# A graph attention layer on one core: queries projected inside the walk instead of ahead of it

## The chip, the core and the metric

The kernel runs on one core of a Trainium2 chip, one launch, all tensors in float32 in device memory. The metric is device time in microseconds (us) from launch to end. The core has five engines that run their own instruction queues in order: TensorE (PE in the profile, with its weight loads as PEld), VectorE (DVE), ScalarE (ACT), GpSimd (POOL) and SyncE (SP, which here only issues transfers). They meet through semaphores.

## What is computed

One pre-normalised graph attention layer over 12500 nodes with 256 features, 8 heads of 32, and 200000 edges sorted by destination:

```python
h = jnp.maximum(_layernorm(x, axis=-1), 0.0)          # 12500 x 256
q, k, v = h @ Wq + bq, h @ Wk + bk, h @ Wv + bv       # each 8 heads of 32
logits = einsum('ehd,ehd->eh', q[dst], k[src]) / sqrt(32)
expv = exp(logits - segment_max(logits, dst)[dst])
agg = segment_sum(expv / segment_sum(expv, dst)[dst] * v[src], dst)
out = agg + (h @ Wskip + bskip)
y = h + gelu(out)
return x + layernorm(y) * gamma + beta
```

The destinations are drawn as `12500 * u**2` and sorted, so low nodes have many edges and high nodes few: 383 edges in a row span up to 26 nodes in the first half of the list and up to 53 in the second.

## The kernel before

**Projection** (`project`, L112). The nodes are cut into 98 blocks of 128 rows, taken in 14 groups of 7. For a block the statistics are made on DVE, the centred and clipped rows are transposed on PE (L95) and copied to SBUF by ACT (L97), and PE multiplies them with `[Wk Wv]` (L161, 512 columns) and with `Wq` (L164, 256 columns). DVE scales the two results by the row's reciprocal deviation and adds the bias (L167, L169). A group's rows go to the device-memory tables `kv_tab` (2 KB a row), `q_tab` (1 KB a row) and `st_tab` (L172).

**Plan** (`make_plan`, L291). Beside the projection, mostly on DVE, the edge list is cut into `S` = 8 streams of about 25000 edges and each stream into `NST` = 66 steps of 384 edges (`K` = 3 pieces of 128, one edge of overlap). Out come the gather indices `idx`, the first node of every step and stream (`d0_row`), rows from which one-hot matrices are made (`e_tab`), penalties for the maxima (`pen_tab`), and a list of output blocks in the order in which they become complete (`slot_row`, two blocks make a pair, 52 pairs). A flag says whether the data fit: no step of a stream may reach further than its window (64 nodes, `WN`), and a block must be complete when its pair is due. If they don't fit, another branch (`walk_partitions`) does the work.

**Walk** (`walk_streams`, L542 on). One loop of 66 steps; each step takes 384 edges of each of the 8 streams. The order on each engine is the order of the program text, written out by hand: `keep` (L559) chains every instruction to the one before it on its engine. The parts of step `c`:

- `prefetch(c+2)` (L789, SP): `et`, `pen`, and for each stream 64 rows of `q_tab` from its first node on, into `qw` (8 loads, L800).
- `gather(c+1, j)` (L803, POOL): 8 indirect transfers for each piece `j`, each of 128 rows of 2 KB from `kv_tab`, into one of five buffers `kv`.
- `hot_e(c+2, i)` (L811) and `hot_n(c+1, j)` (L821): PE multiplies small constants `near`, `near_n` with `et` into the single PSUM buffer `ps_hot`, ACT turns it into the one-hot matrices `to_e` (edges out of nodes) and `to_n` (nodes out of edges).
- `spread` (L831): PE brings each edge its query, `ps_qe`; `times` (L843) multiplies it on DVE with the gathered keys; `total` (L853) sums over each head; `turn` (L861) transposes the logits on PE.
- `maxima` (L871): two scans and a subtraction on DVE, `Exp` on ACT; `turn_back` (L882) transposes the weights on PE; `weigh` (L889) multiplies them on DVE with the values; `weights` (L901) copies on ACT.
- `add_up(c, i)` (L908): PE sums weighted values per node, two streams of 64 nodes to a tile, four tiles; ACT copies the sums to SBUF, SP writes them to `table` (8 writes a step). `carry` (L927): SP moves the last row of each stream on to the next step (4 transfers), where `weigh(c+1, 0)` uses it.
- In most steps, one finished pair (class `Pair`, L598): fetch, norm, transposes (`turn`, L630), skip product (L650: a bias row, then four products of 256 columns), addition of the aggregate (L659), Gelu, statistics, scale, store. Before Gelu, Sqrt and Exp an ACT table is loaded (`table_of`, L781).

**What sets the order around the change.** After `turn_back` PE has, in this order: `hot_e` 0, the pair's addition, `hot_e` 1 to 3, `add_up(c, 0)`, then `spread(c+1, 1, ·)`, for which `times(c+1, 1, ·)` on DVE waits. DVE meanwhile has three `weigh`, `times(c+1, 0, ·)`, `total(c+1, 0)` and the pair's statistics. `hot_e`, `hot_n` and the pair's transposes share `ps_hot`, so each of them must wait until ACT has read the one before.

**Tail** (L1061). Pairs that become due too late for the walk are done after it, one after the other, 8 of them by `FIN_FIRST` = 11 and `FIN_RATE` = 20 (a pair is due in step 11 + m·20/16).

Of the kernel before, what the change touches and what calls it, by code (L numbers as in the profile page):

```python
# [36 lines left out]
P = 128  # L38
# [5 lines left out]
S = 8  # L44
# [4 lines left out]
FIN_FIRST = 11  # L49
FIN_RATE = 20  # L50
PAD = 127.0
IN_RANGE = "every node's number in the tables made on the chip is clamped to the list of nodes"
# [3 lines left out]
def gnn_kernel(ctx: ExitStack, tc: tile.TileContext, x, src, dst, Wq, bq, Wk, bk, Wv, bv,  # L56
# [15 lines left out]
    q_tab = dram.tile([NP + WN, HID], F32, name="q_tab")  # L72
# [7 lines left out]
    b_s = consts.tile([P, HID], F32, name="b_s")  # L80
# [8 lines left out]
    def rows(t, a):  # L89
        nc.scalar.dma_start(t, bass.AP(tensor=a.tensor, offset=a.offset, ap=[[0, P], [1, HID]]))  # L90
# [21 lines left out]
    def project():  # L112

        with tc.tile_pool(name="proj_c", bufs=1) as cpool, \
                tc.tile_pool(name="proj", bufs=2) as pool, \
                tc.tile_pool(name="proj_ps", bufs=2, space=PSUM) as psum:
            w_kv = cpool.tile([P, KC, 2 * HID], F32, name="w_kv")
            w_q = cpool.tile([P, KC, HID], F32, name="w_q")
            for t, w in ((w_kv[:, :, :HID], Wk), (w_kv[:, :, HID:], Wv), (w_q, Wq), (w_s, Wskip)):
                weights(t, w)  # L120
            b_kv = cpool.tile([P, 2 * HID], F32, name="b_kv")
            b_q = cpool.tile([P, HID], F32, name="b_q")
            for t, a in ((b_kv[:, :HID], bk), (b_kv[:, HID:], bv), (b_q, bq), (b_s, bskip),
                         (gam, gamma), (bet, beta)):
                rows(t, a)
            qscale = 1.0 / math.sqrt(D)
            nc.vector.tensor_scalar(b_q, b_q, qscale, None, op0=OP.mult)
            zero = cpool.tile([WN, HID], F32, name="zero")
            nc.vector.memset(zero, 0.0)
            nc.scalar.dma_start(q_tab[NP:, :], zero)  # L130
            for b0 in range(0, NBLK, NB):
                xt = pool.tile([P, NB, HID], F32, name="x_in")
                blocks = min(NB, N // P - b0)
                if blocks < NB:
                    nc.vector.memset(xt[:, blocks, :], 0.0)
# [3 lines left out]
                if blocks < NB and N % P:  # L139
                    nc.sync.dma_start(xt[:N % P, blocks, :], x[(b0 + blocks) * P:, :])  # L140
                mr = pool.tile([P, NB, 2], F32, name="mr")
                norm_stats(pool, xt, mr[:, :, 0], mr[:, :, 1])
                nr = pool.tile([P, NB, 2], F32, name="nr")
# [1281 lines left out]
```

## Time and profile before

| | us |
|---|---|
| median of 11 runs | 2528.29 (2520.78 to 2538.72) |
| the profiled execution | 2520.56 |
| its span, first to last instruction | 2518.7 |
| projection and plan, to the last projected block on DVE | 0 to 346.6 |
| first gather of the walk to the end of the last one | 359.8 to 2388.1 |
| last `weigh` of the walk ends | 2408.3 |
| leftover pairs, first divisor to last scale | 2427.5 to 2511.9 |

| engine | busy us | share |
|---|---|---|
| PE | 1838.1 | 73% |
| DVE | 2055.7 | 82% |
| ACT | 816.3 | 32% |
| POOL | 1579.4 | 63% |

The 16 transfer engines moved 608.30 MB at 242 GB/s. The granted TensorE clock had a mean of 0.798 of full speed. The busy shares are means over three stages with different limits; a group of instructions in the profile is named by its line, engine, output and inputs, with its count, its busy time, the mean of one, and the idle time of the engine just before it with what ended that. "issue" as a releaser means that the engine waited for nothing that the profile shows.

### The profile page before, as it was taken

The numbers are of one execution on the slowest core, as the hardware profiler recorded it, in microseconds if no ns is written. First come the engines' busy times: TensorE is split into PE (matmuls) and PEld (weight loads), VectorE is DVE, ScalarE is ACT, GpSimd is POOL, SyncE is SP. The second block draws the span as 40 slices with busy tenths as digits, with TensorE's granted clock in tenths as the row PEclk, the third lists the DMA queues.
The fourth block names the chain that finished last, engine by engine and source line by source line (L and its number), as shares of the span: only waits on it lengthen the run. The fifth ranks groups of instructions, "written<-read, shape, count | busy, mean of one in ns | idle before, by whom it ended". The sixth has DMA issues, their size and how long they took to land. (4 is left out here: it accounts for less than half of the span.)

```text
span 2518.7 us, 32531 instructions
## 1 busy us (share of the span) xinstructions
PE 1838.1 (73%) x9087; PEld 1017.6 (40%) x9087; DVE 2055.7 (82%) x2501; ACT 816.3 (32%) x1642; POOL 1579.4 (63%) x1629
## 2 busy tenths in 40 slices
PE   5799965666667767777777777777777777777755
PEld 3455532333334434343443334434344343443433
DVE  6689847777778888898888988989888898898844
ACT  0011112222224434344343433434344343443434
POOL 0200027777777777777777777777777777777701
PEclk9899986777777878788777877878788787787866
DMA  6767658888888888888888888988888888888822
GB/s 171 178 169 199 207 171 238 252 253 254 252 262 265 263 271 268 269 266 263 267 267 271 266 261 271 278 269 268 266 265 267 269 268 266 265 263 270 251 63 59
DMA packets 338786, 608.30 MB, mean 242 GB/s; under 512 B 76665, under 2 KB 223155, under 8 KB 338465
## 3 DMA queue, kind: packets, MB, share of 16 engines
q0 software_dynamic: 127872, 418.56, 55.1%
q1 hardware_dynamic: 209781, 186.73, 25.3%
q8 instruction: 74, 1.21, 0.2%
q10 hardware_dynamic: 944, 0.85, 0.2%
q14 instruction: 115, 0.94, 0.1%
HBM read 512.26 MB, written 93.13 MB: 240 GB/s over the span
## 5 line engine op out<-in xcount | busy, mean ns | idle before, releaser
L806 POOL DMA_INDIRECT kv<-kv_tab,idx x1584 | 1546.1, 976 | 489.8 <-issue 436.0
L848 DVE TENSOR_TENSOR prod<-ps_qe,kv 128x1024 f32<-128x1024 f32 x396 | 472.1, 1219 | 187.9 <-DMA kv<-kv_tab,idx 155.0
L838 PE MATMUL ps_qe<-qw,to_e 64*128 64x256 f32 x3168 | 529.1, 472 | 128.0 <-DVE prod L848 127.9
L918 PE MATMUL ps_a<-vw,to_n 128*64 128x264 f32 x3168 | 513.9, 460 | 119.8 <-ACT vw L905 99.2
L893 DVE TENSOR_TENSOR vw<-ps_w,kv 128x2048 f32<-128x2048 f32 x198 | 446.8, 2284 | 98.4 <-PE ps_w L886 95.6
L838 PEld LDWEIGHTS ps_qe<-qw,to_e 64*128 64x128 f32 x3168 | 350.8, 230 | 323.2 <-DVE prod L848 226.3
L857 DVE TENSOR_REDUCE L<-prod 128x64 f32<-128x2048 f32 x198 | 452.7, 2286 | 6.8
L918 PEld LDWEIGHTS ps_a<-vw,to_n 128*64 128x64 f32 x3168 | 223.1, 155 | 453.9 <-issue 195.2
L922 ACT COPY sums_w<-ps_a 128x264 f32<-128x264 f32 x264 | 99.8, 378 | 508.7 <-PE ps_a L918 498.6
L816 PE MATMUL ps_hot<-et,near 48*128 48x384 bf16 x264 | 107.6, 408 | 184.2 <-ACT to_e L818 159.4
L818 ACT ACTIVATE to_e<-ps_hot,ones 128x384 f32<-128x384 f32 x264 | 152.0, 576 | 180.0 <-PE ps_hot L816 157.0
L161 PE MATMUL ps_kv<-w_kv,hT 128*128 128x512 f32 x392 | 194.5, 620 | 19.0 <-ACT hT L97 12.4
L828 ACT ACTIVATE to_n<-ps_hot,ones 128x512 f32<-128x512 f32 x198 | 135.8, 686 | 214.3 <-PE ps_hot L826 199.5
L783 ACT ACT_TABLE_LOAD x131 | 168.1, 1283 | 2.4
L656 PE MATMUL ps_a<-w_s,hT 128*128 128x256 f32 x352 | 138.6, 563 | 0.1
L580 POOL IOTA piece_of<- 3x2 f32 x1 | 0.1, 127 | 197.5 <-issue 197.5
L826 PE MATMUL ps_hot<-near_n,et 48*128 48x512 bf16 x198 | 84.1, 425 | 33.7 <-ACT hT L637 27.6
L656 PEld LDWEIGHTS ps_a<-w_s,hT 128*128 128x128 f32 x352 | 94.5, 281 | 32.8 <-issue 13.9
L97 ACT COPY hT<-ps_t 128x256 f32<-128x256 f32 x98 | 31.7, 375 | 233.9 <-PE ps_t L95 233.8
L161 PEld LDWEIGHTS ps_kv<-w_kv,hT 128*128 128x128 f32 x392 | 71.9, 194 | 81.2 <-issue 49.0
L164 PE MATMUL ps_q<-w_q,hT 128*128 128x256 f32 x392 | 101.2, 381 | 0.0
L167 DVE SCALAR_TENSOR_TENSOR kvo<-ps_kv,mr,b_kv 128x512 f32<-128x512 f32 x98 | 72.4, 738 | 30.6 <-PE ps_kv L161 29.9
(234 smaller groups left out, 1574.2 us busy)
## 6 DMA issues: line engine op xcount, KB each, us to landing
table<-sums_w SPq DMA_DIRECT2D x528, 65.0 KB
qw<-q_tab SPq DMA_DIRECT2D x528, 64.0 KB
kv<-kv_tab,idx POOLq DMA_INDIRECT x1584
kv_tab<-kvo SPq DMA_DIRECT2D x14, 1792.0 KB
sums<-table SPq DMA_DIRECT2D x104, 132.0 KB
x_f<-in_x_dram SPq DMA_DIRECT2D x104, 128.0 KB
out_dram<-o SPq DMA_DIRECT2D x104, 128.0 KB
pen<-pen_tab SPq DMA_DIRECT2D x66, 192.5 KB
```

The costliest lines, as they stand in the source:

```text
L161: nc.tensor.matmul(ps_kv, hT[:, c, :], w_kv[:, c, :], start=c == 0, stop=c == KC - 1)
L656: self.keep(nc.tensor.matmul(self.ps[:, b, :], self.hT[:, b, c, :], w_s[:, c, :], start=False, stop=False, skip_group_check=True))
L783: keep(nc.scalar.activation(dummy[:, 1:2], dummy[:, 0:1], function))
L806: nc.gpsimd.indirect_dma_start(out=t[:, s, :], out_offset=None, in_=kv_tab[:, :], in_offset=bass.IndirectOffsetOnAxis(ap=idx[:, s, j, c:c ...
L816: keep(nc.tensor.matmul(ps[:, :CH], flat[:, i * P:(i + 1) * P], step[c]["et"], start=True, stop=True))
L818: keep(nc.scalar.activation(step[c]["to_e"][:, i, :], ps[:, :CH], AF.Relu, scale=-1.0, bias=ones))
L828: keep(nc.scalar.activation(step[c]["to_n"][:, j, :], ps, AF.Relu, scale=-1.0, bias=ones))
L838: keep(nc.tensor.matmul(ps[:, b, a, :], g["to_e"][r, 2 * half + a, j * P:(j + 1) * P], g["qw"][r, 2 * half + a, :], start=True, stop=True))
L848: keep(nc.vector.tensor_tensor(g["prod"][:, four, :].rearrange("p (a b) d -> p a b d", a=2), g["qe", half].rearrange("p b a d -> p a b d") ...
L857: keep(nc.vector.tensor_reduce(g["L"][:, j, :].rearrange("p (s h) -> p s h", s=S), g["prod"].rearrange("p s (h d) -> p s h d", h=HEADS), A ...
L893: keep(nc.vector.tensor_tensor(t[:, :, :HID].rearrange("p s (h d) -> p s h d", h=HEADS), wj[:, :, :, None].to_broadcast([P, S, HEADS, D]), ...
L918: keep(nc.tensor.matmul(ps[b * WN:(b + 1) * WN, :], g["to_n"][:, j, s * WN:(s + 1) * WN], g["vw"][j][:, s, :], start=j == 0, stop=j == K - ...
```

## The change

The queries are no longer made ahead of the walk. `project` stores the normalised, clipped rows in `h_tab` (ACT makes them: Relu with scale and bias) and only keys and values are projected; its groups grow and shrink at the ends (1, 2, 4, then 7 each, 4, 2, 1 blocks), and the first block of `x` is loaded ahead of the weights. In the walk each step loads windows of `h_tab` three steps ahead (`windows`), transposes them on PE (`turn_windows`), and projects them (`queries`: a bias row from three BF16 pieces, then the products with `w_q`, which holds the scale) into `qw`. Streams 0 to 3 now have windows of 32 nodes and share one tile, so there are three tiles of 128 rows instead of four; the plan's test allows them a reach of less than 31. `near`, `near_n` are built ahead of the branch. `hot_n` of a step moves into that step, the Sqrt table load moves behind `add_up(c, 0)`. The carry has four groups of rows instead of two. Partial output blocks stand at the start of a stream instead of its end, pairs are due at 10 + m·39/32, and the 6 leftover pairs are emitted in three overlapped stages.

```diff
+NARROW = {0: 0, 2: 32, 1: 64, 3: 96}
+WNN = 32
-FIN_FIRST = 11
-FIN_RATE = 20
+FIN_FIRST = 10
+FIN_RATE = 39
...
     def project():
+        sizes = [1] * NBLK
+        if NBLK >= 14:
+            mid = NBLK - 14
+            sizes = [1, 2, 4] + [7] * (mid // 7) + [mid % 7] * (mid % 7 > 0) + [4, 2, 1]
...
+            x_in = [load(0, sizes[0])]
...
+            for t, w in ((w_kv[:, :, :HID], Wk), (w_kv[:, :, HID:], Wv)):
+                weights(t, w)
...
+                if g == 2:
+                    for t, a in ((gam, gamma), (bet, beta)):
+                        rows(t, a)
+                    for t, w in ((w_q, Wq), (w_s, Wskip)):
+                        weights(t, w)
+                    qscale = 1.0 / math.sqrt(D)
+                    nc.vector.tensor_scalar(w_q, w_q, qscale, None, op0=OP.mult)
+                    pieces(b_q3, bq, qscale)
+                    pieces(b_s3, bskip, 1.0)
...
+                    nc.scalar.activation(h[:, b, :], xt[:, b, :], AF.Relu, scale=nr[:, b, 1:2],
+                                         bias=nr[:, b, 0:1])
...
-                    for c in range(KC):
-                        nc.tensor.matmul(ps_q, hT[:, c, :], w_q[:, c, :], start=c == 0,
-                                         stop=c == KC - 1)
-                    rs = mr[:, b, 1:2]
-                    nc.vector.scalar_tensor_tensor(kvo[:, b, :], ps_kv, rs, b_kv, op0=OP.mult,
-                                                   op1=OP.add)
-                    nc.vector.scalar_tensor_tensor(qo[:, b, :], ps_q, rq[:, b:b + 1], b_q,
-                                                   op0=OP.mult, op1=OP.add)
-                for tab, t in ((q_tab, qo), (kv_tab, kvo), (st_tab, nr)):
+                    nc.vector.tensor_tensor(kvo[:, b, :], ps_kv, b_kv, op=OP.add)
+                for tab, t in ((h_tab, h), (kv_tab, kvo), (st_tab, nr)):
...
+        def where(s):
+            return (0, NARROW[s], WNN) if s in NARROW else (s // 2 - 1, s % 2 * WN, WN)
...
-            g["qw"] = early.tile([P, S // 2, HID], F32, name="qw")
+        def windows(c):
+            hw = step[c]["hw"] = hold.tile([P, 3, HID], F32, name="hw")
             for s, node in enumerate(nodes(c)):
-                keep(nc.sync.dma_start(g["qw"][s % 2 * WN:(s % 2 + 1) * WN, s // 2, :],
-                                       q_tab[ds(node, WN), :]))
+                i, at, w = where(s)
+                keep(nc.sync.dma_start(hw[at:at + w, i, :], h_tab[ds(node, w), :]))
+        def turn_windows(c, part):
+            g = step[c]
+            tiles = (range(1), range(1, 3))[part]
+            ps = hot_ps.tile([P, 2, KC, P], F32, name="ps_hot")[:, :len(tiles)]
+            for b, i in enumerate(tiles):
+                for k in range(KC):
+                    keep(nc.tensor.transpose(ps[:, b, k, :], g["hw"][:, i, k * P:(k + 1) * P],
+                                             ident))
+            g["hwT"] = hold.tile([P, 2, KC, P], F32, name="hwT", bufs=1)[:, :len(tiles)]
+            keep(nc.scalar.copy(g["hwT"], ps))
+        def queries(c, part):
+            g = step[c]
+            if part == 0:
+                g["qw"] = hold.tile([P, 3, HID], F32, name="qw")
+            tiles = (slice(0, 1), slice(1, 3))[part]
+            n = tiles.stop - tiles.start
+            ps = hot_ps.tile([P, 2, HID], F32, name="ps_hot")[:, :n]
+            keep(nc.tensor.matmul(ps, one_row, b_q3[:, :n], start=True, stop=False,
+                                  skip_group_check=True))
+            for b in range(n):
+                for k in range(KC):
+                    keep(nc.tensor.matmul(ps[:, b, :], g["hwT"][:, b, k, :], w_q[:, k, :],
+                                          start=False, stop=k == KC - 1, skip_group_check=True))
+            keep(nc.scalar.copy(g["qw"][:, tiles, :], ps))
...
-                step[c]["to_n"] = hot.tile([P, K, S * WN], F32, name="to_n")
+                step[c]["to_n"] = hot.tile([P, K, n], F32, name="to_n", bufs=1)
...
-                g["sums"] = work.tile([P, S // 2, SUMS], F32, name="sums_w")
+                g["sums"] = work.tile([P, 3, SUMS], F32, name="sums_w", bufs=1)
+            streams = [s for s in range(S) if where(s)[0] == i]
             ps = ag_ps.tile([P, 2 * HID], F32, name="ps_a")[:, :SUMS]
             for j in range(K):
-                for b in range(2):
-                    s = 2 * i + b
-                    keep(nc.tensor.matmul(ps[b * WN:(b + 1) * WN, :],
-                                          g["to_n"][:, j, s * WN:(s + 1) * WN],
+                for s in streams:
+                    _, at, w = where(s)
+                    keep(nc.tensor.matmul(ps[at:at + w, :],
+                                          g["to_n"][:, j, i * P + at:i * P + at + w],
                                           g["vw"][j][:, s, :], start=j == 0, stop=j == K - 1,
...
+            for r, tiles, streams in ((31, slice(0, 1), slice(0, 1)), (95, slice(0, 1), slice(1, 2)),
+                                      (63, slice(0, 3), slice(2, 8, 2)),
+                                      (127, slice(0, 3), slice(3, 8, 2))):
+                row = sums[r:r + 1, tiles, :]
+                keep(nc.sync.dma_start(kv[0:1, streams, HID:], row[:, :, :HID]))
+                keep(nc.sync.dma_start(w[0:1, streams, :], row[:, :, HID:]))
...
             if c:
-                add_up(c - 1, S // 2 - 1)
+                add_up(c - 1, 2)
                 carry(c - 1)
             if c + 2 < NST:
                 prefetch(c + 2)
+            if c + 3 < NST:
+                windows(c + 3)
...
-                    hot_n(c + 1, half)
+                hot_n(c, half)
...
-            if more:
-                hot_n(c + 1, 2)
+            hot_n(c, 2)
             if pair:
                 pair.skip()
+            if c + 2 < NST:
+                turn_windows(c + 2, 0)
             maxima(c)
...
             weigh(c, 0)
             if more:
                 gather(c + 1, 2)
-            if c + 2 < NST:
-                hot_e(c + 2, 0)
             if pair:
                 pair.add()
             if c + 2 < NST:
-                hot_e(c + 2, 1)
+                queries(c + 2, 0)
+                hot_e(c + 2, 0)
             if pair:
                 pair.gelu()
-                table_of(AF.Sqrt)
             if c + 2 < NST:
+                turn_windows(c + 2, 1)
+                hot_e(c + 2, 1)
+                queries(c + 2, 1)
                 hot_e(c + 2, 2)
                 hot_e(c + 2, 3)
...
                 add_up(c, 0)
+                if pair:
+                    table_of(AF.Sqrt)
...
-        for m in rest:
...
+        for i in range(len(pairs) + 2):
+            if i < len(pairs):
+                pair = pairs[i]
+                pair.fetch()
...
+            if 0 < i <= len(pairs):
+                pair = pairs[i - 1]
+                pair.skip()
+                pair.add()
+                pair.gelu()
+            if i > 1:
+                pair = pairs[i - 2]
+                pair.stats()
...
```

## The prediction

> **What bounds the kernel now.** Three stages have three limits, so I read stage by stage: the costliest groups first, then the order of time inside a step, then the clock in the same stretch.
>
> The costliest groups of instructions, the whole execution:
>
> ```profile
> L806 POOL DMA_INDIRECT kv<-kv_tab,idx x1584 | 1546.1, 976 | 489.8 <-issue 436.0
> L848 DVE TENSOR_TENSOR prod<-ps_qe,kv 128x1024 f32<-128x1024 f32 x396 | 472.1, 1219 | 187.9 <-DMA kv<-kv_tab,idx 155.0
> L656 PE MATMUL ps_a<-w_s,hT 128*128 128x256 f32 x352 | 138.6, 563 | 0.1
> L164 PE MATMUL ps_q<-w_q,hT 128*128 128x256 f32 x392 | 101.2, 381 | 0.0
> ```
>
> POOL issues 1584 gathers; its idle time is 0.30 us before each, nearly all of it waiting for nothing ("issue"). 0.95 + 0.30 = 1.25 us, times 24 gathers, is 30.0 us a step, and from 359.8 to 2388.1 us 66 steps take 30.7 each. So **the walk is paced by POOL's issuing**, and DVE waits for its gathers (155.0 us).
>
> The order of time in a step with a pair (start, length, engine):
>
> ```profile
> 1223.03 0.60 PE L652 MATMUL ps_a<-b,one_row 3*128 3x512 bf16 x1
> ...
> 1223.56 3.69 PE L656 MATMUL ps_a<-w_s,hT 128*128 128x256 f32 x8
> ...
> 1227.18 0.40 PE L886 MATMUL ps_w<-ident,W 64*128 64x64 f32 x3
> ...
> 1227.68 1.13 PE L661 MATMUL ps_a<-o,ident 128*128 128x256 f32 x4
> ...
> 1229.11 0.58 ACT L818 ACTIVATE to_e<-ps_hot,ones 128x384 f32<-128x384 f32 x1 [0.74 <-PE ps_hot L816]
> ...
> 1229.74 0.32 PE L816 MATMUL ps_hot<-et,near 48*128 48x384 bf16 x1 [0.67 <-ACT to_e L818]
> ...
> 1232.61 1.15 PE L918 MATMUL ps_a<-vw,to_n 128*64 128x264 f32 x4
> ...
> 1241.32 2.35 DVE L848 TENSOR_TENSOR prod<-ps_qe,kv 128x1024 f32<-128x1024 f32 x2
> ```
>
> Between the end of `turn_back` (1227.58) and `times(c+1, 1, ·)` (1241.32) DVE is busy with its own work for 13.7 us. In that time PE must finish `hot_e`, the addition, `add_up(c, 0)` and the first `spread(c+1, 1, ·)`; each use of the one `ps_hot` buffer costs a hand-over of 0.67 us. In a step without a pair (`turn_back` ends 460.81, `times` 472.34) that cover is 11.5 us. This is where the change puts new PE work.
>
> The same stretch in windows of 2 us (busy time of the engines, then granted clock, transfer share, GB/s):
>
> ```profile
> 1228.00:1230.00 2.00, 1.33 (x6) 0.58 (x5) 2.00 (x3) 1.25 (x3) 1.39 (x3) 1.00 0.94 252
> 1230.00:1232.00 2.00, 0.06 (x1) 0.00 (x0) 2.00 (x2) 1.97 (x4) 1.58 (x2) 0.61 0.94 316
> 1232.00:1234.00 2.00, 1.55 (x5) 0.29 (x4) 2.00 (x2) 0.74 (x2) 1.50 (x2) 0.50 0.97 346
> 1234.00:1236.00 2.00, 1.26 (x6) 0.77 (x8) 2.00 (x3) 0.33 (x2) 1.39 (x3) 0.50 0.83 227
> ```
>
> The clock is full or half; from 1228 to 1242 its mean is 0.63. In windows of 0.5 us over 300 us of the walk it changes only at multiples of 3.4 us: to full after a stretch in which PE was busy 0.93 or more, to half after one below 0.70 (one exception at 0.60).
>
> The projection, two blocks:
>
> ```profile
> 334.47 1.98 PE L161 MATMUL ps_kv<-w_kv,hT 128*128 128x512 f32 x4 [0.21 <-ACT hT L97]
> ...
> 336.29 1.03 PE L164 MATMUL ps_q<-w_q,hT 128*128 128x256 f32 x4
> ...
> 337.15 1.88 PE L161 MATMUL ps_kv<-w_kv,hT 128*128 128x512 f32 x4
> ```
>
> PE runs without gaps: the `Wq` product holds it 337.15 - 336.29 = 0.86 us a block, and PE is busy 47.6 of 50 us in the stretch 200 to 250. **The projection is paced by PE.**
>
> **Projection.** 98 blocks x 0.86 = 84.3 us leave PE. DVE loses `qo` (46.6 us in all) and the clipping (29.5), which ACT takes over as Relu (0.55 each by L620's 1.09 for two, 98 x 0.55 = 54 us, under PE's 2.2 us a block). The first product started at 25.2 us, behind four weights and a first group of 7 blocks; with one block first I estimate 12: 13 us more. The smaller last groups shorten the landing of the tables, but `near` and `near_n` are now two chains instead of one (7.7 us from 351.1 to 358.8), and the first gather still waits behind them: I count 0. The plan's work stays beside it on DVE, with the pieces of `bq` (3.5 us as at 347.1) added. Together 97 us. Bounds: the stage moves 62 MB (the sum of its windows); at 213 GB/s, its best window, it can't end before 291 us, which leaves a gain near 50; at the walk's 268 GB/s it is 232 us and hides. With the tables' landing (9 us from 346.6 to 355.5) gained too it is 106. I take 97, as 213 GB/s was what was asked for there, at a share of 0.78.
>
> **Transfers, tables, small copies.** 384 rows of 1 KB instead of 512 for the windows, 376 rows of sums instead of 504: 0.26 MB of some 8 MB a step. Nothing, as POOL's issuing hides it; SP still issues 8 windows (5.2 us) and 8 sums. The carry grows from 4 to 8 transfers of 0.6 us: 2.5 us more on SP, ahead of `et` and the windows. Behind it wait `weigh(c+1, 0)` (7 us of room: carry over at 1218.6, `weigh` 1227.6, less 2 for landing) and `hot_e(c+2, 0)` (`et` issued 1218.7, used 1227.4): hidden, but little is left. `hot_n` in its new step keeps its place on PE and ACT and is shorter by 128 of 512 columns; with a single `to_n` it follows `add_up(c-1, 2)`, which PE has issued by then. One `sums_w` copy (0.38 us) goes.
>
> **New PE work behind `turn_back`.** A list for a step with a pair, full clock / half clock: addition 1.1 / 1.9 (1.13 at full); `queries` 0, half of the bias and skip rows' 0.53 + 3.69 = 4.22 at half clock, 1.1 / 2.1; `queries` 1, all of it, 2.1 / 4.2; four transposes 0.60 / 1.06 (L95, L634); four `hot_e` at 0.33 / 0.48; `add_up(c, 0)` 1.6 / 3.1 (12 instructions 1.56; 1.15 + 2.03 at half); half of a `spread`, 8 instructions, 1.1 / 2.1. Sum 8.9 / 16.3. Hand-overs: five of 0.67 and one of 0.48 (a 256-column copy, 0.375): 3.8. So the first `spread` is ready **12.7 us after `turn_back` at full clock, 20.2 at half**, against a cover of 13.7. Without a pair 11.6 / 18.3 against 11.5. The only solid piece is `queries` 1, 4.2 us, too short to hold a whole 3.4 us stretch in most cases; I take three quarters of the way to half clock, as the mean of 0.63 has it: 18.3 and 16.6.
>
> `add_up(c, 0)` now has 24 instructions of 32 columns. Today's two 64-column halves run two abreast (four take 1.15 at half clock, about two of 0.44 and a tail), so four abreast cost what twelve cost now; if they don't, it is 1.6 to 3.1 more. I take four abreast, as the order by pairs does not hinder two.
>
> [...]
>
> Also, `turn_windows(c+2, 0)` stands ahead of `Exp` in ACT's queue and of `turn_back` in PE's: two transposes and a copy, 0.5 + 0.4 + 0.1 = 1.0 us later in a step with a pair, where `skip` ends last; about 0.5 without.
>
> Against this stands what DVE waits for gathers today, which a late DVE simply eats: 31.0 us in 16.2 steps from 1000 to 1500, 1.9 each; 4.05 (and 4.67) in steps without pairs, 4.3. Per step: 18.3 - 13.7 + 1.0 - 1.9 = 3.7 us in 46 steps with pairs, 170; 16.6 - 11.5 + 0.5 - 4.3 = 1.3 in 18 steps, 23. **Walk +193 us.** POOL then waits for `kv` buffers that `weigh` frees late. Bounds: full clock, nothing (POOL keeps its 30.7 us); half throughout, 5.6 x 46 + 3.0 x 18 = 312.
>
> [...]
>
> **Tail.** 84.4 us for 8 pairs, 10.5 each; 6 are left: -21. Each is a chain from `norm` to the statistics that read `h`, which still has one buffer, so the overlap can save little: DVE holds the statistics up to 1.2 us behind a divisor that waits for its fetch, 6 x 1.2 = 7. Together 28; bounds 21 and 44 (PE's 6.7 us a pair).
>
> **Sum**, on the profiled execution: 2520.6 - 97 + 193 - 28 = 2589; the median of the runs stands 7.7 us above it, so 2528.3 + 68 = **2596 us**.
>
> **Rivals.**
> *PE's work fits.* The price is 0 if the first `spread` is ready within 13.7 + 1.9 - 1.0 = 14.6 us. For it: 12.7 at full clock, and a fuller PE earns full clock more often. Against: the hand-overs keep the stretch below 0.93. Time 2528 - 97 - 28 = 2403.
> *The 32-column products don't run four abreast.* 2.7 us more a step at that clock: 6.4 x 46 + 4.0 x 18 = 366, time 2769. For it: each product has two passes on one tile; against: two tiles run abreast today.
> *Transfers take PE's place in the projection:* gain 50, time 2643, inside the range.
> *The plan falls to the other branch:* by the reference's data the first four streams reach 26 nodes at most, under 31, so no chance.
>
> **Chances.** My forecast 0.54 (its own range 2525 to 2690), fitting 0.30, not four abreast 0.10; the rest lies between. The range leaves out most of the 2769 case and little below 2403: 2395 to 2700. About 0.2% (5 us) is what can't be told from no change: faster 0.31, within 0.04, slower 0.65.
>
> **What would show it.** Right: POOL's gathers showing waits for DVE, DVE waiting at L848 for `ps_qe` (or `spread`'s line) 4 to 5 us a step where it waited for `kv`, walk steps of 33 to 35 us, a first gather near 263. Wrong: POOL still at 1.25 us a gather to the end; a clock near 1.00 behind `turn_back`; `add_up` of the first tile at 3 us or more; a first gather later than 300.

## The result, and the profile after

The changed kernel takes 2588.5 us (median of 8 runs) against 2527.5: a ratio of **1.0239** (95% interval 1.0224 to 1.0254). The prediction said 2596. The profiled execution took 2575.8 us, its span 2574.0. The first gather and the end of the last `weigh` cut both spans into three parts:

| part of the span | before | after | difference | predicted |
|---|---|---|---|---|
| to the first gather | 359.8 | 278.9 | -80.9 | -97 |
| walk, to the end of the last `weigh` | 2048.6 | 2205.7 | +157.1 | +193 |
| behind it | 110.3 | 89.4 | -20.9 | -28 |

The costliest groups of the changed kernel, the whole execution:

```profile
L924 POOL DMA_INDIRECT kv<-kv_tab,idx x1584 | 1549.5, 978 | 633.2 <-issue 425.9
L1012 DVE TENSOR_TENSOR vw<-ps_w,kv 128x2048 f32<-128x2048 f32 x198 | 446.9, 2285 | 229.0 <-DMA kv<-sums_w 177.6
L967 DVE TENSOR_TENSOR prod<-ps_qe,kv 128x1024 f32<-128x1024 f32 x396 | 467.4, 1219 | 196.4 <-PE ps_qe L957 156.7
...
L957 PE MATMUL ps_qe<-qw,to_e 64*128 64x256 f32 x3168 | 450.5, 421 | 1.5 <-DVE prod L967 1.5
...
L1038 PE MATMUL ps_a<-vw,to_n 128*32 128x264 f32 (+1 forms) x3168 | 378.4, 487 | 19.3 <-ACT vw L1024 11.9
...
L934 PE MATMUL ps_hot<-et,near 48*128 48x384 bf16 x264 | 110.3, 418 | 265.5 <-DMA et<-e_tab 105.1
```

POOL no longer paces the walk: 207 of its 633 us of idle time are waits. DVE waits for the spread (156.7), as forecast. But its longest wait is another: 177.6 us of `weigh` (`vw`, L1012) for the **carry**, the last row of sums that SP copies into `kv`. Before, `weigh` waited 98.4 us, nearly all for PE, never for the carry:

```profile
L893 DVE TENSOR_TENSOR vw<-ps_w,kv 128x2048 f32<-128x2048 f32 x198 | 446.8, 2284 | 98.4 <-PE ps_w L886 95.6
```

The longest wait need not be the one that ends last; the table behind experiment 12 sorts that out.

The order of time in one step of the changed kernel (start, length, engine); L1055 and L1056 are the carry, L1005 is `turn_back`, L1012 `weigh`, L934 `hot_e`:

```profile
1203.98 1.56 PE L1038 MATMUL ps_a<-vw,to_n 128*64 128x264 f32 x12
...
1205.58 0.38 ACT L1042 COPY sums_w<-ps_a 128x264 f32<-128x264 f32 x1 [1.96 <-PE ps_a L1038]
...
1206.84 0.59 SPq L1055 DMA_DIRECT2D kv<-sums_w  x1
...
1207.48 1.02 SPq L1056 DMA_DIRECT2D wden<-sums_w  x1
...
1208.59 0.53 SPq L1055 DMA_DIRECT2D kv<-sums_w  x1
...
1209.17 0.65 SPq L1056 DMA_DIRECT2D wden<-sums_w  x1
...
1210.00 0.70 SPq L1055 DMA_DIRECT2D kv<-sums_w  x1
...
1210.75 0.65 SPq L1056 DMA_DIRECT2D wden<-sums_w  x1
...
1211.57 0.65 SPq L1055 DMA_DIRECT2D kv<-sums_w  x1
...
1212.49 0.58 PE L1005 MATMUL ps_w<-ident,W 64*128 64x64 f32 x3 [2.37 <-ACT W L999]
...
1212.84 0.64 SPq L1056 DMA_DIRECT2D wden<-sums_w  x1
...
1213.59 0.34 SPq L880 DMA_DIRECT2D et<-e_tab  x1
...
1215.64 2.29 DVE L1012 TENSOR_TENSOR vw<-ps_w,kv 128x2048 f32<-128x2048 f32 x1 [3.75 <-DMA et<-e_tab]
...
1216.55 0.50 PE L934 MATMUL ps_hot<-et,near 48*128 48x384 bf16 x1 [1.15 <-DMA et<-e_tab]
```

The weights for `weigh` are ready at 1213.07; the carry's last transfer into `kv` starts at 1211.57 and lands at 1215.47, and `weigh` starts at 1215.64. (The view names `et`, which shares a semaphore with a transfer of the carry; `et` lands at 1216.51, and the first `hot_e` follows it.) In the 15 steps between 1000 and 1500 us `weigh` starts 2.6 us behind `turn_back` on average, before 0.05. The carry's issue, up to the last transfer into `kv`, takes 7.0 us there; before, 2.1 us, and then 6.9 us passed until `weigh`. The same queue delivers `et` late to PE (105.1 us of waits at L934).

Why do eight issues of 0.65 us take 7 to 10 us? The view of waits, SP's queue of the changed kernel (total, times, longest):

```profile
SPq L1056 <- DMA table<-sums_w: 77.9, 75, 3.4
...
SPq L1055 <- DMA table<-sums_w: 33.0, 57, 2.1
...
SPq L1055 <- DMA kv<-kv_tab,idx: 24.0, 44, 0.8
```

SP waits for the stores of sums that it issued just before. (It also waits for gathers into the same `kv`, but it does so for 38.9 us in experiment 7, which loses no time.) The list of compiled instructions with their semaphores (DMAHW: SP's own transfers; DMASW: the gathers) says why:

```
1248 L1045 DMACopy table<-sums_w 63x264 [waits DMAHW6_49]
1249 L1055 DMACopy kv<-sums_w 1x16x16 [waits DMAHW7_49,DMASW5_49]
1250 L1056 DMACopy wden_2003<-sums_w 1x8x1 [waits DMAHW0_49]
1251 L1055 DMACopy kv<-sums_w 1x16x16 [waits DMAHW1_49,DMASW6_49]
```

Eight semaphores take turns, so here **each transfer of SP waits until the one eight places before it has landed**: in the trace 2199 of 2210 transfers of SP use the semaphore of the one eight places before, and all but one start behind its landing. With a carry of four, its transfers stood eight places behind the first four stores of sums, which had landed by then: SP had no wait for a store there. With eight, the carry stands eight places behind all eight stores, and these land late (experiment 7).

### The profile page after: what moved, and what is told of

Its sections match the earlier page's. It is cut to its first block, busy times and chain, and to the rows that moved or that the text cites. A ratio compares the mean times of both kernels' runs of the same rounds, so it can differ in the third digit from the quotient of the medians.

```text
span 2574.0 us, 35233 instructions
## 1 busy us (share of the span) xinstructions
PE 1910.8 (74%) x10015; PEld 1097.0 (43%) x10015; DVE 1990.0 (77%) x2316; ACT 945.8 (37%) x1950; POOL 1584.4 (62%) x1639
## 5 line engine op out<-in xcount | busy, mean ns | idle before, releaser
L1012 DVE TENSOR_TENSOR vw<-ps_w,kv 128x2048 f32<-128x2048 f32 x198 | 446.9, 2285 | 229.0 <-DMA kv<-sums_w 177.6
L967 DVE TENSOR_TENSOR prod<-ps_qe,kv 128x1024 f32<-128x1024 f32 x396 | 467.4, 1219 | 196.4 <-PE ps_qe L957 156.7
L957 PE MATMUL ps_qe<-qw,to_e 64*128 64x256 f32 x3168 | 450.5, 421 | 1.5 <-DVE prod L967 1.5
L1038 PE MATMUL ps_a<-vw,to_n 128*32 128x264 f32 (+1 forms) x3168 | 378.4, 487 | 19.3 <-ACT vw L1024 11.9
L917 PE MATMUL ps_hot<-w_q,hwT 128*128 128x256 f32 x792 | 331.9, 582 | 0.0
L934 PE MATMUL ps_hot<-et,near 48*128 48x384 bf16 x264 | 110.3, 418 | 265.5 <-DMA et<-e_tab 105.1
L917 PEld LDWEIGHTS ps_hot<-w_q,hwT 128*128 128x128 f32 x792 | 215.7, 290 | 125.4 <-issue 80.4
L1038 PEld LDWEIGHTS ps_a<-vw,to_n 128*32 128x32 f32 (+1 forms) x3168 | 152.6, 139 | 228.8 <-issue 52.7
L919 ACT COPY qw<-ps_hot 128x256 f32<-128x256 f32 (+1 forms) x132 | 63.2, 479 | 395.9 <-PE ps_hot L917 395.9
L947 ACT ACTIVATE to_n<-ps_hot,ones 128x384 f32<-128x384 f32 x198 | 114.2, 577 | 82.7 <-PE ps_hot L945 81.8
L934 PEld LDWEIGHTS <-near 48*128 48x128 bf16 x264 | 25.6, 97 | 255.1 <-DMA et<-e_tab 133.8
L900 PE MATMUL ps_hot<-ident,hw 128*128 128x128 f32 x396 | 89.6, 349 | 58.2 <-ACT to_e L936 43.8
L903 ACT COPY hwT<-ps_hot 128x256 f32<-128x256 f32 (+1 forms) x132 | 63.2, 479 | 148.3 <-PE ps_hot L900 145.8
L985 PE MATMUL ps_x<-ident,L 128*64 128x128 f32 x198 | 57.6, 291 | 65.3 <-DVE L L976 62.7
```

The source lines that it names most:

```text
L917: keep(nc.tensor.matmul(ps[:, b, :], g["hwT"][:, b, k, :], w_q[:, k, :], start=False, stop=k == KC - 1, skip_group_check=True))
L934: keep(nc.tensor.matmul(ps[:, :CH], near[:, i * P:(i + 1) * P], step[c]["et"], start=True, stop=True))
L947: keep(nc.scalar.activation(step[c]["to_n"][:, j, :], ps, AF.Relu, scale=-1.0, bias=ones))
L957: keep(nc.tensor.matmul(ps[:, b, a, :], g["to_e"][r, 2 * half + a, j * P:(j + 1) * P], g["qw"][r, (half + a) * half, :], start=True, stop= ...
L967: keep(nc.vector.tensor_tensor(g["prod"][:, four, :].rearrange("p (a b) d -> p a b d", a=2), g["qe", half].rearrange("p b a d -> p a b d") ...
L1012: keep(nc.vector.tensor_tensor(t[:, :, :HID].rearrange("p s (h d) -> p s h d", h=HEADS), wj[:, :, :, None].to_broadcast([P, S, HEADS, D]), ...
```

## Experiments

Times are medians of each run's own comparison; "before" was 2526 to 2530 us beside the runs of the first three groups. "Walk" is taken from one profile each, as above; experiment 4, which leaves the walk as it is, shows 2198 in place of 2206, so some 10 us between two walks say little. In the expectations theory A is the prediction's (PE's work behind `turn_back` paces the step), theory B the carry.

**1. The carry's order.** `carry` and `prefetch` are split in two: the transfers into `kv` first, then `et`, then those into `wden`, then `pen`:

```diff
-                carry(c - 1)
-            if c + 2 < NST:
-                prefetch(c + 2)
+                carry(c - 1, 0)
+            if c + 2 < NST:
+                prefetch(c + 2, 0)
+            if c:
+                carry(c - 1, 1)
+            if c + 2 < NST:
+                prefetch(c + 2, 1)
```

> The changed kernel, with one order altered on SP's queue: the four transfers of the carry into kv first, then et, then the four into wden, then pen. Theory A (the one of the prediction: PE's work behind turn_back paces the step, the wait of weigh for the carry only lies beside it): DVE starts weigh about 2.5 us earlier and then waits those 2.5 us longer for the first spread; only what PE idles for et today (105 us in the whole walk) can come back, so 2560 to 2590 us. Theory B (the carry of eight transfers paces the step: DVE starts weigh 1.3 to 2.5 us after its transfers' end in every step, some 2.6 us behind turn_back): the wait of weigh falls from 178 us in all to under 40, the spread's wait stays near 157, the walk is 120 to 150 us shorter: 2440 to 2470 us.

Measured: 2541.0 us, ratio 1.0069 (1.0039 to 1.0098), walk 2165. Between the two. `weigh` still waits 208.4 us for the carry: the four `kv` transfers alone take 5.7 us to issue. Fewer of them did not make them quick. PE's wait for `et`, which now has four transfers ahead of it in place of eight, fell from 105.1 to 53.3 us, and the walk by 41.

**2. Queries back in the projection.**

```diff
-                for tab, t in ((h_tab, h), (kv_tab, kvo), (st_tab, nr)):
+                    nc.vector.scalar_tensor_tensor(qo[:, b, :], ps_q, qscale, b_q, op0=OP.mult,
+                                                   op1=OP.add)
+                for tab, t in ((q_tab, qo), (kv_tab, kvo), (st_tab, nr)):
...
-            if c + 2 < NST:
-                turn_windows(c + 2, 0)
...
-                queries(c + 2, 0)
...
-                turn_windows(c + 2, 1)
-                queries(c + 2, 1)
```

> The changed kernel with its queries put back into the projection: Wq is multiplied there again, the walk loads 32- and 64-row windows of the finished q table two steps ahead, and turn_windows and queries are gone; the 32-column tiles and the carry of eight transfers stay. Theory A (PE's work behind turn_back): DVE's wait for the first spread goes, and the walk returns to POOL's 30.7 us a step, 157 us shorter, while the projection gets its 84 us of Wq back: 2500 to 2530 us. Theory B (the carry): the wait of weigh behind the carry stays at 2 to 3 us a step and with it a walk at most 60 us shorter than that of the changed kernel: 2600 to 2670 us.

Measured: 2602.8 us, ratio 1.0305 (1.0284 to 1.0326), first gather at 355.7, walk 2147. Its groups:

```profile
L971 DVE TENSOR_TENSOR vw<-ps_w,kv 128x2048 f32<-128x2048 f32 x198 | 446.9, 2285 | 299.0 <-DMA kv<-sums_w 264.7
...
L926 DVE TENSOR_TENSOR prod<-ps_qe,kv 128x1024 f32<-128x1024 f32 x396 | 467.7, 1218 | 69.1 <-DMA kv<-kv_tab,idx 60.3
```

Without PE's new work the spread's wait is gone, and the carry's takes its place (177.6 to 264.7). The walk is only 58 us shorter, as theory B forecast; what theory A said would return to POOL's pace did not. That the carry's wait ends last in the changed kernel too does not follow from this.

**3. Both edits.**

> Both edits at once: queries in the projection, and the carry's transfers into kv and et ahead of those into wden. Both theories expect a walk paced by POOL again, 30.7 us a step and 2490 to 2530 us; A expects no difference from the run with the queries alone put back, B expects it 80 to 150 us faster than that run.

Measured: 2596.1 us, ratio 1.0264 (1.024 to 1.0288), walk 2151. Both theories missed by over 65 us: putting `kv` first does not help here at all, and `weigh` waits 238.8 us for the carry. So neither PE's work nor the number of transfers ahead explains the carry's delay; what SP's queue shows in their place are its waits for the stores (185 us at the `kv` transfers, in the view of waits).

**4. Three buffers for `h` behind the walk.**

```diff
-            self.h = self.pool.tile([P, 2, HID], F32, name="h", bufs=1)
+            self.h = self.pool.tile([P, 2, HID], F32, name="h", bufs=self.hb)
```

> The changed kernel with three buffers in place of one for h in the pairs behind the walk. If the one h keeps the three stages from overlapping (the reading of the trace: norm of the next pair starts right behind the addition that reads h, and a pair takes 10.3 us as before), a pair falls to 7 to 8 us (PE has 6.7 us of work in each) and the time by 10 to 20 us: 2568 to 2578. If something else holds the pairs apart (the load of the tables of functions, the fetches), no change: 2585 to 2592.

Measured: 2565.2 us, ratio 1.0179 (1.013 to 1.0228); the stretch behind the walk takes 74.0 us in place of 89.4 (one of the four runs took 2586.5). In the changed kernel's trace (order of time) the next pair's `h` starts the moment the addition that reads the last one is over:

```profile
2511.93 0.68 DVE L804 TENSOR_TENSOR sums<-sums,h 128x512 f32<-128x512 f32 x1
...
2512.65 1.09 ACT L753 ACTIVATE h<-x_f,mr_f 128x256 f32<-128x256 f32 x2 [2.29 <-DVE sums L804]
```

A pair takes 10.3 us, as before. The three stages did not overlap until `h` had buffers.

**5. SP's queue rearranged in the changed kernel.** The carry goes ahead of the third tile's two stores, and rows 31 and 95 in one transfer:

```diff
-            for r, tiles, streams in ((31, slice(0, 1), slice(0, 1)), (95, slice(0, 1), slice(1, 2)),
-                                      (63, slice(0, 3), slice(2, 8, 2)),
-                                      (127, slice(0, 3), slice(3, 8, 2))):
...
+            keep(nc.sync.dma_start(put[:, 0:2, :], sums[31:P:64, 0:1, of]))
+            for r, streams in ((63, slice(2, 8, 2)), (127, slice(3, 8, 2))):
+                keep(nc.sync.dma_start(put[:, streams, :], sums[r:r + 1, :, of]))
...
-                carry(c - 1)
-            if c + 2 < NST:
-                prefetch(c + 2)
+                carry(c - 1, 0)
+            if c + 2 < NST:
+                prefetch(c + 2, 0)
+            if c:
+                carry(c - 1, 1)
+                stores(c - 1, 2)
+            if c + 2 < NST:
+                prefetch(c + 2, 1)
```

> The changed kernel with SP's queue rearranged at the head of a step: the carry goes ahead of the two stores of the third tile's sums, its kv part in three transfers (rows 31 and 95 in one), then et, then three for wden, then the two stores. The queries stay in the walk. Each transfer of SP waits until the one eight places before it has landed; here the carry's kv transfers no longer stand eight places behind the stores just issued. Theory B (the carry paces the step): the kv transfers take 2 to 2.5 us in place of 7.0, weigh starts at turn_back again, the spread's wait stays near 157 us or less, the walk falls from 2206 to 2050 to 2080 us, and the time to 2420 to 2460. Theory A (PE's work behind turn_back paces the step as soon as the carry does not): weigh's wait goes, but the spread's grows to 220 to 330 us, the walk takes 2100 to 2170 us, the time is 2475 to 2550.

Measured: **2461.9 us**, ratio 0.9756 (0.972 to 0.9791), walk 2082. Its groups:

```profile
L927 POOL DMA_INDIRECT kv<-kv_tab,idx x1584 | 1556.5, 983 | 503.9 <-issue 445.5
L970 DVE TENSOR_TENSOR prod<-ps_qe,kv 128x1024 f32<-128x1024 f32 x396 | 466.3, 1217 | 220.2 <-PE ps_qe L960 201.4
L1015 DVE TENSOR_TENSOR vw<-ps_w,kv 128x2048 f32<-128x2048 f32 x198 | 446.7, 2283 | 82.6 <-PE ps_w L1008 51.7
```

An order on one queue, with two transfers fewer, is worth 124 us of the walk's 157. POOL is back near its own pace (58 us of its idle time are waits; its issuing alone takes 30.3 us of a step of 31.2). The spread's wait grew to 201.4 us, as theory A said, yet the walk is near B's figure.

**6. The same order with the queries in the projection.**

> The same rearrangement of SP's queue in the kernel whose queries are back in the projection. Nothing is left then that either theory could make the step wait for: POOL's 30.7 us a step and a walk of 2030 to 2060 us for both, first gather near 357, 2485 to 2520 us in all. If the walk stays above 2100 us, a third cause is at work, since the order without this rearrangement gave 2147.

Measured: 2507.2 us, ratio 0.9918 (0.9887 to 0.9949), walk 2072, first gather at 357.1. As both expected, but for a walk 12 us over; `weigh` still waits 122.6 us for the carry.

**7. The kernel before with a carry of eight.**

```diff
-                sums = step[c]["sums"][r:r + 1, :, :]
+                for i in (0, 2):
+                    sums = step[c]["sums"][r:r + 1, i:i + 2, :]
```

> The kernel before with one edit: its carry's four transfers are split into eight of half the size, in the same place. Theory B: the last kv transfer starts 2.6 us later or more and waits besides for the landing of the stores eight places before it; of the 7.0 us that lie between the last kv transfer and weigh some 3 to 5 are used up, in the steps with the least room all of it; weigh waits for the carry in a third of the steps or more, and the walk grows by 20 to 100 us: 2545 to 2630 us. Theory A: the carry is hidden, no change: 2520 to 2535.

Measured: 2528.1 us, ratio 0.9999 (0.9986 to 1.0012), walk 2060. Theory B as stated missed, theory A's figure came: eight transfers alone cost nothing. The carry's first four transfers on SP's queue, in the order of time of this kernel:

```profile
1213.57 0.68 SPq L934 DMA_DIRECT2D kv<-sums_w  x1
1214.29 0.61 SPq L935 DMA_DIRECT2D wden<-sums_w  x1
1215.00 0.56 SPq L934 DMA_DIRECT2D kv<-sums_w  x1
1215.62 0.55 SPq L935 DMA_DIRECT2D wden<-sums_w  x1
```

And in experiment 2, the same view:

```profile
1210.98 0.76 SPq L1014 DMA_DIRECT2D kv<-sums_w  x1
1212.46 0.72 SPq L1015 DMA_DIRECT2D wden<-sums_w  x1
1216.08 0.52 SPq L1014 DMA_DIRECT2D kv<-sums_w  x1
1219.08 0.66 SPq L1015 DMA_DIRECT2D wden<-sums_w  x1
```

Both carry eight, neither projects queries in the walk; only in the second SP stands still for 3 us between issues. What differs most ahead of them are the stores, eight in both: of 63 rows each, or four of 31 and four of 63. From the records of each transfer's completions in the two traces (1000 to 1500 us; medians, a step's stores in their order):

| stores of a step | completions recorded | issue to landing, us |
|---|---|---|
| experiment 7: eight of 63 rows | 10 each | 3.9 4.0 3.9 3.8 3.9 3.9 4.0 4.1 |
| changed kernel: four of 31, four of 63 | 2 and 10 | 4.4 5.4 7.8 10.5 9.4 9.2 6.4 6.9 |
| experiment 2: the same | 2 and 10 | 4.4 5.4 7.8 10.6 11.3 10.7 9.4 9.9 |

(128 rows show 16, three rows 4.) Each store of 31 rows lands 1.5 to 3.3 us behind the last, and the four stores of 63 rows that follow land late too (6.4 to 11.3 us). Why the counts are 2 and 10 no run here shows.

The trace's records of single rows on their way tell how the four stores of 31 rows go. Up to the first store of 63 rows, in the 14 steps between 1000 and 1500 us with no fetch of sums beside them, the changed kernel's rows start 0.044 us apart and at most two are under way at once (four in one step), although all four stores had been issued. In the kernel before 8 to 11 rows are under way at once, and with stores of 32 rows (experiment 11) 14. The author reads this as four stores that go over one and the same transfer engine, with the carry behind them; the records of rows do not name an engine, so that is an estimate from these numbers.

**8. Experiments 4 and 5 together.**

> The two edits that gained, together: SP's queue rearranged at the head of a step, and three buffers for h in the pairs behind the walk. They touch different stages, so the gains add: the stretch behind the walk falls from 89 to 74 us, and the time from 2462 to 2440 to 2450 us. If the pairs gained by something that the rearranged walk also gives (a fuller clock, fewer transfers under way), less: 2455 to 2462.

Measured: **2440.8 us**, ratio 0.9669 (0.9649 to 0.9688), 75.0 us behind the walk. The gains add; this version beats both kernels.

**9. Queries left out** of experiment 5's kernel; the normalised rows stand in for them:

```diff
-            hw = step[c]["hw"] = hold.tile([P, 3, HID], F32, name="hw")
+            hw = step[c]["qw"] = hold.tile([P, 3, HID], F32, name="qw", bufs=4)
...
-                queries(c + 2, 0)
...
-                queries(c + 2, 1)
```

> The kernel with SP's queue rearranged, with the queries left out: the windows' normalised rows are used as queries as they are, so Wq, its bias and the transposes of the windows are not computed at all, neither in the projection nor in the walk; everything else is the same. This prices PE's work behind turn_back when the carry does not pace the step. Theory A (it costs what DVE waits for the spread, 201 us in the whole walk): the walk ends at POOL's pace, 2035 to 2050 us in place of 2082, 2415 to 2430 us in all, and the spread's wait goes. Theory B (it lies beside POOL's issuing): the spread's wait goes and a wait for kv's gathers takes its place, the walk stays within 15 us of 2082 and the time at 2447 to 2465.

Measured: 2436.0 us, ratio 0.9635 (0.9617 to 0.9653), walk 2068. B's kind, with a time between the two: the spread's wait is replaced (this kernel's groups, several releasers each),

```profile
L942 DVE TENSOR_TENSOR prod<-ps_qe,kv 128x1024 f32<-128x1024 f32 x396 | 469.7, 1218 | 118.2 <-DMA kv<-kv_tab,idx 106.4 <-PE ps_qe L932 3.8 <-PE ps_a L1013 0.7
...
L987 DVE TENSOR_TENSOR vw<-ps_w,kv 128x2048 f32<-128x2048 f32 x198 | 446.8, 2284 | 166.6 <-DMA kv<-sums_w 109.5 <-PE ps_w L980 44.1 <-DMA table<-sums_w 8.0
```

by the gathers' and the carry's. All of PE's new work costs 14 us of walk, 26 of the time, against a kernel that then waits for its carry instead.

**10. Only the two stores behind the carry.**

```diff
                 carry(c - 1)
+                stores(c - 1, 2)
```

> The changed kernel with one order altered: the two stores of the third tile's sums stand behind the carry in place of ahead of it; the carry keeps its eight transfers, kv and wden in turn, and et stays behind them. If the carry is late by its place (two issues ahead of it, and each of its transfers waiting for the landing of the one eight places before), weigh's wait falls by a third to a half and the time to 2510 to 2555 us. If it is late by its number alone, eight issues of 0.65 us with et behind them, the two stores' 0.9 us are all there is: 2555 to 2585 us.

Measured: 2563.7 us, ratio 1.0149 (1.0117 to 1.018), walk 2191. The time is the second reading's, though `weigh`'s wait fell by a third (229.0 to 152.3 us), as the first had it: the spread's wait took that over (156.7 to 226.6), for `et` lands as late as before. The carry's issue even grew, from 7.0 to 9.0 us: now its third to sixth transfer stand eight places behind the four 31-row stores. In experiment 5 only the third `kv` transfer does.

**11 and 12. Stores of 32 and 64 rows**, in the changed kernel and in experiment 8's:

```diff
-                keep(nc.sync.dma_start(table[s, ds(g["nodes"][s], w - 1), :],
-                                       g["sums"][at:at + w - 1, i, :]))
+                keep(nc.sync.dma_start(table[s, ds(g["nodes"][s], w), :],
+                                       g["sums"][at:at + w, i, :]))
```

> The changed kernel with one edit: a step stores 32 and 64 rows of each tile's sums in place of 31 and 63 (the last row is the unfinished sum of a node that the next step's store writes again, so the result is the same). In the changed kernel's trace a store of 31 rows counts two completions, one of 63 rows ten, one of 128 rows sixteen, and the four 31-row stores of a step land 4.4, 5.4, 7.8 and 10.5 us after their issue where the 63-row stores of the kernel before land after 3.8: as if each ran whole on one and the same transfer engine, with the carry's rows behind them. Theory D (that is what makes the carry late): all stores land in about 4 us, SP no longer waits for them between the carry's transfers (111 us), weigh's wait falls from 229 us to under 110, the walk from 2206 to 2070 to 2120 us, the time to 2455 to 2510. Theory N (the carry is late by its eight issues and its place alone): 2570 to 2590.

> The same edit in the kernel with SP's queue rearranged and three buffers for h behind the walk. There the carry hardly paces the step any more (weigh waits 91 us in the whole walk, 43 of them for PE), POOL issues its gathers at 31.2 us a step: theory D expects weigh's wait for the carry (37 us) to go and the time to fall by 0 to 20 us, 2420 to 2441; theory N expects no change, 2436 to 2446.

Measured: 3878.9 us, ratio 1.0129 (1.0088 to 1.0171), and 3833.5 us, ratio 0.9993 (0.9971 to 1.0015). Both ran on a chip on which the kernel before itself takes 3837 us. Its limit is another: DVE waits 23.5 us a step at the first products, for something that the view names only `remote`; by its place it is the gathers, which is not shown (the groups of experiment 11):

```profile
L967 DVE TENSOR_TENSOR prod<-ps_qe,kv 128x1024 f32<-128x1024 f32 x396 | 468.3, 1219 | 1592.9 <-remote 1554.5
```

So these times decide nothing between D and N. The traces show only that 32 and 64 rows count 16 completions, that the fourth store of a step lands as soon as the first (1.46 and 1.49 us; with transfers at 152 GB/s in place of 228), and that SP does not wait for a store in the carry of experiment 11 any more (111 us in the changed kernel). This fits D. What the 31 rows alone are worth in time stays **open**.

**Which wait ends last, over all runs.** Means over a step of each trace, 65 steps (59 to 64 for `et` and `hot_e`), in us from the end of `turn_back`; a negative number is ahead of it. "Products" is the first `times(c+1, 1, ·)`, "idle" DVE's wait just before it, "rest" the time from there to the next `turn_back`.

| kernel | `et` lands | first `hot_e` starts | `weigh` starts | first `spread` ready | products start | idle | rest | step |
|---|---|---|---|---|---|---|---|---|
| before | -2.6 | 1.1 | 0.0 | 11.1 | 13.0 | 0.0 | 17.8 | 30.8 |
| changed | 3.8 | 4.1 | 2.6 | 18.3 | 18.4 | 2.8 | 14.7 | 33.1 |
| 1, `kv` then `et` | 2.8 | 3.5 | 2.5 | 17.6 | 17.7 | 1.9 | 14.8 | 32.5 |
| 10, two stores behind | 3.8 | 4.1 | 1.4 | 18.1 | 18.2 | 3.7 | 14.7 | 32.9 |
| 5, queue rearranged | -0.4 | 2.8 | 0.3 | 16.4 | 16.4 | 3.1 | 14.8 | 31.2 |
| 2, queries ahead | 4.7 | 5.1 | 3.9 | 14.9 | 16.9 | 0.0 | 15.4 | 32.3 |
| 9, no queries | -0.2 | 2.2 | 1.6 | 12.7 | 14.7 | 0.0 | 16.4 | 31.1 |

The products start at the later of two: when the first `spread` is ready, or 13 us behind `weigh`'s start, which is DVE's own work. In the changed kernel the spread ends last: 2.6 + 13.0 is 15.6, but the spread is ready at 18.3, and DVE idles in 61 of 65 steps. So `weigh`'s wait for the carry, the longest in the profile, is covered there. Experiment 10 shows it: `weigh` starts 1.2 us sooner, `et` does not land sooner, and the step is 0.2 us shorter. In the four kernels with queries in the walk the rest is 14.7 or 14.8, and the step follows the spread.

SP's late queue reaches the spread through `et`, which stands behind the carry. With `et` landing 3.8 us behind `turn_back`, PE starts its first `hot_e` 1.2 us later than in experiment 5; the remaining 0.7 us of the spread's delay come behind it, where the clock plays a part: from `turn_back` to the spread its mean is 0.66 in place of 0.71. `add_up`, which needs `weigh`'s result, hardly waits for it (L1038 above). With the queries out of the walk (2 and 9) the carry ends last instead.

## Why the prediction came out, step by step

Time, direction and the wait that ends last in a step (DVE for the first `spread`) were right. Two terms behind the number were not, with opposite signs, and that they nearly cancel is luck: SP's queue, counted as nothing, is worth 124 of the walk's 157 us, and the slack that takes up PE's lateness was nearly twice what was counted.

**Projection, -97 forecast, -81 measured.** Experiment 2, with `Wq` multiplied there again, has its first gather at 355.7: `Wq` is worth 77 us (forecast 84), everything else at the start 4 (forecast 13). The first product starts at 17.9, not 12. From 25 to 100 us PE is busy 58.9 of 75 us at a transfer share of 1.00 and more: that fits the rival "transfers take PE's place" for this stretch alone, and was not tested.

**"Transfers, tables, small copies. Nothing" is the step that failed.** It priced the carry's four more transfers at 2.5 us of SP's issuing and called both `weigh` and `hot_e`, which stand behind them, hidden. It counted bytes and issues. It did not look at what each transfer waits for, nor at the shape of the stores: 31 rows land up to 10.5 us after their issue where 63 took 3.8, and the carry waits for them in the turn of eight semaphores. The 7 us of room were read in a single step; on average 6.9 us pass between the carry's last issue into `kv` and `weigh`, 3 of them for landing. `weigh` starts 2.6 us late, and `et` lands 3.8 us behind `turn_back`, where it used to be 2.6 ahead. Rearranging SP's queue gives back 124 of the walk's 157 us.

**PE's work behind `turn_back`, +193 forecast.** The forecast had the first `spread` ready 18.3 us after `turn_back` with a pair, 16.6 without; measured are 18.2 (45 steps) and 18.6 (20). That is partly luck, as `et`'s lateness is in the measured figure: in experiment 5 they are 15.9 and 17.3. Put into the working, these give 1.3 x 46 + 2.0 x 18 = 96 us; measured are 33 over the kernel before, 14 against the same kernel without queries. The slack makes the difference. By the table the rest of a step is 3.1 us shorter than before, mostly as DVE waits less for gathers (155.0 us at this instruction before, 32.6 now); the working had 0.9 with a pair and 3.8 without (what DVE waits for gathers, less 1.0 or 0.5), 1.7 on average. So a step is 5.4 us late at the products and saves 3.1: 2.3 us, 153 of the 157. With SP's queue rearranged it is 3.4 less 3.0. Of the signs named, steps of 33 us came; the wait for `ps_qe` was 2.4 us a step, not 4 to 5.

The two waits of DVE lie side by side, so the gains do not add: without the queries the walk gains 58, with SP's queue rearranged 124, with both 137.

**The clock.** The working's reading of it is looser than it says. Between 900 and 2300 us of the kernel before, the clock went to full after stretches of 3.4 us with PE busy 0.88 or more (71 times), and to half after 0.73 or less (72 times); but 20 stretches below 0.70 kept full clock, where the working names one exception. From `turn_back` to the first `spread` the mean is 0.66 in the changed kernel, near the 0.63 that it took.

**`add_up(c, 0)` on 32 columns:** abreast, as assumed. In the changed kernel they start in fours within 0.02 us; eight of them take 0.66 us and sixteen 1.10 at full clock, twenty-four 2.87 at half, where twelve of 64 columns take 1.56 at full clock. The rival of 2769 us falls.

**Behind the walk, -28 forecast, -21 measured:** the two pairs fewer, and no overlap. The prediction saw the one buffer of `h` and still counted 7 us; experiment 4 shows that it allowed none.

**The rival "PE's work fits" (2403 us)**: its condition, a first `spread` within 14.6 us, does not hold even with SP's queue rearranged (16.4), but the price is small there, 33 us of walk. The best version here stands 38 us above it.

## What to carry to other kernels

For every transfer that a change adds or reshapes, ask what it waits for, where on its queue it stands, and how long transfers of its shape take to land (here 31 rows up to 10.5 us, 63 rows 3.8), not only how many bytes and issues it has. When a profile names one wait, try the change that removes it and look for the wait that takes its place: here two waits covered each other, and the longer was the one that cost nothing until the other was gone. An order on a queue that looks like housekeeping was worth more than all the arithmetic that was moved.

## What the runs showed that was not expected

- The same 3168 products of the spread take 450.5 us in the changed kernel and 529.1 before. One takes 387 ns at full clock and 667 at half in the changed kernel; the mean granted clock while they run is 0.93, before 0.85. PE is busy 1910.8 us there in place of 1838.1; that this raised the clock was not shown.
- Four stores of 32 KB, a small part of a step's 8 MB, held up a queue: the 63-row stores behind them land after 9.4 us in place of 3.8.
- One chip ran the unchanged kernel in 3837 us in place of 2527, and the two kernels traced there wait 23.5 us a step at the first products; stores landed in 1.5 us there. Why is open.
